# A two-layer graph attention network: TensorE takes four rows of each part of the largest tile in layer 1, and layer 2's row buffer grows from 38 to 41 rows

## The chip, the cores and the metric

The kernel runs on one core of a Trainium2 chip. The metric is the device time of one execution in microseconds (us); less is better. TensorE is written PE (its weight loads PEld), VectorE DVE, ScalarE ACT, GpSimd POOL and SyncE SP, as in the profile.

## The reference

10,000 nodes with 768 numbers each, 160,000 random edges and a loop on each node, sorted by target. Two layers of graph attention, each with a layer norm and a second product added, then a last norm over input plus output. The attention is the same in both layers; layer 1 has 4 heads of 256 numbers, layer 2 one head of 768.

```python
xl = (x @ W).reshape(n, heads, out_ch)
alpha_src = jnp.einsum('nhc,hc->nh', xl, a_src)
alpha_dst = jnp.einsum('nhc,hc->nh', xl, a_dst)
e = jax.nn.leaky_relu(alpha_src[src] + alpha_dst[dst], 0.2)
m = jax.ops.segment_max(e, dst, num_segments=n)
e = jnp.exp(e - m[dst])
s = jax.ops.segment_sum(e, dst, num_segments=n)
alpha = e / (s[dst] + 1e-16)
msg = xl[src] * alpha[:, :, None]
out = jax.ops.segment_sum(msg, dst, num_segments=n)
...
h = gat_conv(x, edge_index, W1, a_src1, a_dst1, b1, HEADS, HID, True)
h = jax.nn.relu(layer_norm(h, g1, be1)) + (h0 @ Wr1 + br1)
h1 = h
h = gat_conv(h, edge_index, W2, a_src2, a_dst2, b2, 1, OUT_DIM, False)
h = layer_norm(h, g2, be2) + (h1 @ Wr2 + br2)
```

All numbers are 32-bit floats. The output is the norm of x plus the last h.

## The kernel before

**Nodes in tiles.** The nodes are sorted by their number of edges and cut into 79 tiles of 128. A tile has as many slots as its largest node may have edges, by a rule from the sizes alone (`slot_counts`): the largest tile 41, the next 27, 26, 25 and so on down to 8. A node's edges fill its slots from the front; what is left over points at a row that adds nothing. The tiles are worked on in the order `TURNS`: every second one from the smallest up, then the others down again. By position in that order the slots are 8, 10, 11, 12, 12, 13, ... up to 26 at position 38, 41 at position 39, then 27, 25, 24, 23, 22, 22, 21, 21, 20, 20, 20, 19, 19, 19, 18, ... down to 9 at position 78. Positions 25 to 28 have 19 slots, 29 to 31 have 20, 32 and 33 have 21. There are 1,377 slots in all; `FIRST[t]` is the first slot of position t.

**The ring.** Each layer has a table of one row a node in main memory: in layer 1 the product and its logits, 1,033 numbers with the rank; in layer 2 770 numbers. One slot of one tile is fetched by one gather (L424), an indirect DMA on POOL that brings 128 rows. It lands in a ring buffer (`Ring`, L440): slot q lies in place q modulo the ring's size, 29 places in layer 1, 38 in layer 2. `fetch(upto)` issues the gathers up to a slot; after row k of a tile has been used, the loops call `fetch(FIRST[t] + k + 1 + size)`. A gather waits until the old row in its place has been read by everything that reads it. In layer 1, gathers beyond the first ring leave out slots that point at no row. In layer 2 the first slot of each tile is the tile's own rows, and is loaded from SP's queue instead (L452).

**Orders.** Both layers run under a manual schedule: each engine works through its instructions in the order in which the program writes them. So a matmul that is written later stands behind all that is written earlier for PE, and the same for the other engines and queues.

**Layer 1** (`ordered_layer1`, L667). A tile whose slots fit the ring is whole: one set of weights over all its rows (`logits`, `normalised`), then PE adds the first `ON_PE1` = 4 rows or fewer (L719: a diagonal matrix per row and head on ACT; L725: the matmul of it with the row), and DVE adds the others to the same accumulator in PSUM. Of four such rows one is multiplied and added by DVE alone (L519, four instructions, one a head), three are multiplied by ACT (L508, four instructions) and added by DVE (L515). Meanwhile PE transposes, makes the product of this tile's x (L171) and the tile before's product for layer 2 (L803). The tile at position 39 has 41 slots, more than 29, so `attend_parts` (L522) takes it in three parts of 13, 14 and 14 rows: weights of a part, the accumulator and the sum scaled down to the new maximum (L541), then its rows, one in four by DVE alone and three by ACT and DVE. PE takes no part. Before the call, `due(n)` has the rest of the tile before written out, with its product for layer 2. Next comes a division (`divided`, L435).

**Layer 2** (`ordered_layer2`, L846). In a whole tile DVE adds columns 0 to 511 of each row (L519), and PE adds columns 512 to 767 for all rows (L891: one diagonal per row on ACT, in 5 buffers of 4; L892: the matmul). PE also has the second product of each tile (`residual`, L903 and L906). The weights of the next tile are made within the loop over this one's rows, at row `turn`, and its diagonals three rows later:

```python
if t + 1 < NT and SLOTS[t + 1] + LEAD <= ring.size:
    ahead = weights_of(t + 1)
    turn = min(max(n // 3, n + SLOTS[t + 1] + 2 * LEAD - ring.size), n - LEAD)
```

`LEAD` is 3. Two norms end each tile (`norms`); their steps are taken in the loop of the following tile, at rows 0, 3, 6 and 9, and each deviation needs a square root from ACT (L565). Position 39, with 41 slots over the ring's 38, goes through `attend_parts` too: DVE adds all 768 columns of each row to an accumulator in SBUF. It is not made ahead of time in position 38, and position 40's weights are not made ahead in it.

Of the kernel before, what the change touches and what calls it, by code (L numbers as in the profile page):

```python
# [35 lines left out]
P = 128  # L36
# [8 lines left out]
LISTS = 4  # L45
G = 4
RING1 = 29
RING2 = 38
LEAD = 3
DIAGONALS = 5  # L50
ON_PE2 = 512
# [28 lines left out]
def gnn_kernel(ctx, tc, x, x_cols, src, dst, src_col, dst_col, W1, a_src1, a_dst1, b1, g1, be1, Wr1, br1,  # L80
# [423 lines left out]
    def multiply(row, e, dh):  # L504

        for h in range(e.shape[1]):
            s = slice(h * dh, (h + 1) * dh)
            nc.scalar.activation(row[:, s], row[:, s], AF.Copy, scale=e[:, h:h + 1])  # L508
# [10 lines left out]
            nc.vector.scalar_tensor_tensor(acc[:, s], row[:, s], e[:, h:h + 1],  # L519
                                           (acc if first is None else first)[:, s], op0=OP.mult, op1=OP.add)  # L520

    def attend_parts(small, ring, acc, h_, ad, bias, heads, dh, t):  # L522

        c = heads * dh
        groups = -(-SLOTS[t] * 2 // ring.size)
        cuts = [FIRST[t] + SLOTS[t] * g // groups for g in range(groups + 1)]
        top = total = None
        nc.vector.memset(acc[:, :c], 0.0)
        for lo, hi in zip(cuts, cuts[1:]):
            e, new = logits(small, ring, lo, hi, ad, heads, c, top)  # L530
            if lo == FIRST[t]:
                doubled(e, t)
            part = small.tile([P, heads], F32, name="part")
            nc.vector.reduce_sum(part, e.rearrange("p k h -> p h k"), axis=AX.X)
            if top is not None:
                fade = small.tile([P, heads], F32, name="fade")
                nc.vector.tensor_sub(fade, top, new)
                nc.scalar.activation(fade, fade, AF.Exp)
                for h in range(heads):
                    s = slice(h * dh, (h + 1) * dh)  # L540
                    nc.vector.tensor_scalar(acc[:, s], acc[:, s], fade[:, h:h + 1], None, op0=OP.mult)  # L541
                nc.vector.tensor_mul(fade, total, fade)
                nc.vector.tensor_add(part, part, fade)
            top, total = new, part
            for q in range(lo, hi):
                shared = heads > 1 and (q - lo) % SHARE
                if shared:
                    multiply(ring.slot(q), e[:, q - lo], dh)
                weigh(acc, ring.slot(q), e[:, q - lo], dh, shared=shared)
                ring.fetch(q + 1 + ring.size)  # L550
        divided(small, h_, acc, total, bias, heads, dh)
# [115 lines left out]
    def ordered_layer1():  # L667
        with tc.tile_pool(name="b1", bufs=1) as pool, tc.tile_pool(name="small1", bufs=2) as small, \
# [33 lines left out]
            def on_pe(t):  # L702


                return min(max(SLOTS[t] // 2 - 5, 1), ON_PE1, SLOTS[t])

            def weights_of(t):

                n, m = SLOTS[t], on_pe(t)
                e, _ = logits(small, ring, FIRST[t], FIRST[t] + n, ring.slot(FIRST[t])[:, C1:C1 + H1], H1, C1)  # L710
                yield e
                normalised(small, e, H1, t)

                acc = ps_acc.tile([P, 2 * BANK], F32, name="acc")
                diagonals = pool.tile([P, ON_PE1 * H1, P], F32, name="diagonals")
                for lo, hi in ((0, min(m, 2)), (min(m, 2), m)):
                    for k in range(lo, hi):
                        for i in range(H1):
                            nc.scalar.activation(diagonals[:, k * H1 + i, :], ident, AF.Copy,  # L719
                                                 scale=e[:, k, i:i + 1])  # L720
                    for k in range(lo, hi):
                        for i in range(H1):

                            c, d = i * DH1, (i + 1) * DH1
                            nc.tensor.matmul(acc[:, c:d], diagonals[:, k * H1 + i, :],  # L725
                                             ring.slot(FIRST[t] + k)[:, c:d],
                                             start=(k == 0 and c % BANK == 0),
                                             stop=(k == m - 1 and (d % BANK == 0 or d == C1)),
                                             skip_group_check=True)
                    yield acc  # L730

            def shared(t, k):
# [21 lines left out]
            for t in range(NT + 1):  # L754
                live, events = t < NT, []
                n = SLOTS[t] if live else 0
                first = done = on_pe(t) if live else 0
                whole = live and n <= ring.size
                if whole and not ready:
                    ahead = weights_of(t)  # L760
                    ready += itertools.islice(ahead, 2)

                def multiplied(upto):
                    nonlocal done
                    while whole and done < min(upto, n):
                        if shared(t, done):
                            multiply(ring.slot(FIRST[t] + done), e[:, done], DH1)
                        done += 1

                if whole:  # L770
                    e, acc = ready
                if last:
                    r_before, means = last
                    stats = deviation(small, pieces(means[:, :C1], BANK))
                for _ in ahead:
                    pass
                if full is not None:
                    store(t - 2)
                moves = []
                if live and t:  # L780
                    xT, moves = from_x(t)
                multiplied(first + 2)
                if last:
                    h = pool.tile([P, C1], F32, name="h")
                    scaled(h, [means[:, :C1]], stats, g1_b, be1_b)
                    nc.vector.scalar_tensor_tensor(h, h, 0.0, r_before[:, :C1], op0=OP.max, op1=OP.add)
                for move in moves:
                    move()
                multiplied(first + LEAD)
                if last:  # L790
                    hT = pool.tile([P, K1, P], F32, name="hT")
                    events = [(first + j, move) for j, move in enumerate(halves(hT, h))]
                if live and t:
                    r = product(xT, wr1, C1, ps_r)

                def to_layer2():
                    nonlocal full
                    nc.sync.dma_start(h1_d[t - 1], hT.rearrange("p k n -> p (k n)"))
                    full = []
                    for c in range(0, R2, BANK):  # L800
                        q = ps_half.tile([P, BANK], F32, name="half")[:, :min(BANK, R2 - c)]
                        for j in range(K1):
                            nc.tensor.matmul(q, hT[:, j, :], w2[:, j, c:c + q.shape[1]],  # L803
                                             start=(j == 0), stop=(j == K1 - 1))
                        full.append((c, q))

                if last:
                    events.append((first + 2, to_layer2))

                def next_x():  # L810
                    nonlocal xt
                    xt = fetch_x(t + 1)

                if t + 1 < NT:
                    events.append((first + 2, next_x))

                def due(k):
                    while events and events[0][0] <= k:
                        events.pop(0)[1]()

                if live and not whole:
                    due(n)
                    acc = ps_acc.tile([P, 2 * BANK], F32, name="acc")
                    ad = small.tile([P, H1], F32, name="ad")
                    nc.vector.tensor_copy(ad, ring.slot(FIRST[t])[:, C1:C1 + H1])
                    attend_parts(small, ring, acc, acc, ad, None, H1, DH1, t)
                ready = []
                ahead = iter(())
                if whole and t + 1 < NT and SLOTS[t + 1] + LEAD <= ring.size:
                    ahead = weights_of(t + 1)  # L830
                for k in range(n if whole else 0):
                    multiplied(k + 1 + LEAD)
                    if n - LEAD <= k < n - LEAD + 2:
                        ready += itertools.islice(ahead, 1)
                    if k >= first:
                        weigh(acc, ring.slot(FIRST[t] + k), e[:, k], DH1, shared=shared(t, k))
                    ring.fetch(FIRST[t] + k + 1 + ring.size)
                    due(k)
                due(DEGREES)
                ready += itertools.islice(ahead, max(2 - len(ready), 0))  # L840
                last = None
                if live:
                    last = r, acc
# [405 lines left out]
```

## Time and profile before

| what | us |
|---|---|
| timed runs, median of three | 5388.15 (5386.93 to 5388.26) |
| the profiled execution's own time | 5386.19 |
| its span | 5384.3 |
| busy: PE / PEld | 4721.3 / 2818.7 |
| busy: DVE / ACT / POOL | 4348.2 / 3138.9 / 3238.2 |
| layer 1, first to last tile (about) | 896 to 3464 |
| layer 2, first weighted row to the end (about) | 3464 to 5372 |
| position 39, layer 1: first weights to end of the division | 2121.2 to 2200.0 |
| position 39, layer 2: first weights to those of position 40 | 4395.8 to 4448.1 |

A line of the profile's groups reads: line of the program, engine, operation, what it writes and reads with shapes, how often; busy time and mean nanoseconds of one; the idle time of the engine just ahead of these, and what ended most of it. A line of an engine's queue (timeline) has the start and length in us, the same names, and in brackets the idle time before it with what ended it. Neighbours alike are merged, with their number behind an x. A line of a table by stretches has the stretch, its length, each engine's busy time with the number of instructions, the clock granted to TensorE, the share of time that the DMA engines were busy, and GB/s.

### The profile page before, as it was taken

The numbers are of one execution on the slowest core, as the hardware profiler recorded it, in microseconds if no ns is written. First come the engines' busy times: TensorE is split into PE (matmuls) and PEld (weight loads), VectorE is DVE, ScalarE is ACT, GpSimd is POOL, SyncE is SP. The second block draws the span as 40 slices with busy tenths as digits, with TensorE's granted clock in tenths as the row PEclk, the third lists the DMA queues.
The fourth block names the chain that finished last, engine by engine and source line by source line (L and its number), as shares of the span: only waits on it lengthen the run. The fifth ranks groups of instructions, "written<-read, shape, count | busy, mean of one in ns | idle before, by whom it ended". The sixth has DMA issues, their size and how long they took to land. (4 is left out here: it accounts for less than half of the span.)

```text
span 5384.3 us, 59633 instructions
## 1 busy us (share of the span) xinstructions
PE 4721.3 (88%) x15011; PEld 2818.7 (52%) x15011; DVE 4348.2 (81%) x8008; ACT 3138.9 (58%) x8204; POOL 3238.2 (60%) x3159
## 2 busy tenths in 40 slices
PE   8999996999999886478999999799988846889998
PEld 3444443555555543245555555466665534556665
DVE  5784244899999888888999999499887876878998
ACT  3434343787888877778888888344433313334443
POOL 3446455455666665556666554367776766767774
PEclk9999998999999998789999999899998978989999
DMA  4333635899999996899999998699999998999995
GB/s 155 126 98 90 90 93 202 307 338 342 359 358 369 358 346 252 306 323 355 359 365 362 350 334 303 221 327 377 369 337 327 332 301 301 341 328 354 369 382 216
DMA packets 474308, 1591.37 MB, mean 296 GB/s; under 512 B 118327, under 2 KB 122487, under 8 KB 473958
## 3 DMA queue, kind: packets, MB, share of 16 engines
q0 software_dynamic: 322384, 1286.62, 66.3%
q1 hardware_dynamic: 149520, 297.43, 16.3%
q10 hardware_dynamic: 2054, 3.42, 0.2%
q8 instruction: 126, 2.06, 0.2%
q14 instruction: 224, 1.84, 0.1%
HBM read 1431.80 MB, written 177.29 MB: 299 GB/s over the span
## 5 line engine op out<-in xcount | busy, mean ns | idle before, releaser
L424 POOL DMA_INDIRECT ring<-table,slots x2675 | 2659.6, 994 | 1486.7 <-DVE acc L519 366.4
L519 DVE SCALAR_TENSOR_TENSOR acc<-ring,e,acc 128x256 f32<-128x256 f32 (+1 forms) x2538 | 1570.8, 619 | 113.3 <-PE acc L725 37.7
L508 ACT ACTIVATE ring<-ring,e 128x256 f32<-128x256 f32 x3320 | 1351.5, 507 | 0.2
L515 DVE TENSOR_TENSOR acc<-acc,ring 128x1024 f32<-128x1024 f32 x830 | 1021.3, 1230 | 80.6 <-ACT ring L508 9.2
L171 PE MATMUL big<-w,xT 128*128 128x512 f32 x1896 | 826.1, 597 | 27.0 <-DMA w<-in_W_dram 9.6
L906 PE MATMUL big<-wr,w 128*128 128x512 f32 (+1 forms) x2528 | 846.4, 488 | 0.0
L892 PE MATMUL big<-ring,diagonals 128*128 128x256 f32 x2672 | 667.2, 412 | 193.3 <-ACT diagonals L891 180.3
L171 PE MATMUL big<-wr,xT 128*128 128x512 f32 x1896 | 835.4, 597 | 0.2 <-ACT xT L688 0.2
L803 PE MATMUL half<-w,hT 128*128 128x512 f32 (+1 forms) x2528 | 830.4, 486 | 0.0
L892 PEld LDWEIGHTS big<-ring,diagonals 128*128 128x128 f32 x2672 | 548.2, 208 | 309.8 <-ACT diagonals L891 211.8
L803 PEld LDWEIGHTS half<-w,hT 128*128 128x128 f32 x2528 | 477.8, 189 | 372.7 <-issue 310.7
L906 PEld LDWEIGHTS big<-wr,w 128*128 128x128 f32 x2528 | 482.6, 191 | 340.1 <-issue 307.5
L725 PE MATMUL acc<-ring,diagonals 128*128 128x256 f32 x1816 | 452.2, 406 | 220.5 <-ACT diagonals L719 220.2
L171 PEld LDWEIGHTS big<-w,xT 128*128 128x128 f32 x1896 | 362.5, 192 | 486.5 <-issue 467.6
L171 PEld LDWEIGHTS big<-wr,xT 128*128 128x128 f32 x1896 | 357.7, 192 | 421.6 <-issue 420.9
L725 PEld LDWEIGHTS acc<-ring,diagonals 128*128 128x128 f32 x1816 | 365.9, 204 | 299.7 <-ACT diagonals L719 242.7
L891 ACT ACTIVATE diagonals<-ident,e 128x128 f32<-128x128 f32 x1336 | 400.5, 387 | 147.6 <-DVE e L499 129.3
L565 ACT ACTIVATE sd<-mv,eps 128x1 f32<-128x1 f32 x237 | 69.8, 295 | 638.0 <-DVE mv L563 637.7
L649 DVE TENSOR_TENSOR scr<-big,ad_b 128x1024 f32<-128x1024 f32 x79 | 96.7, 1224 | 381.6 <-ACT row L646 381.6
L654 POOL TENSOR_TENSOR row<-row,none 128x1024 f32<-128x1024 f32 x79 | 187.0, 2368 | 266.8 <-ACT row L646 266.3
L719 ACT ACTIVATE diagonals<-ident,e 128x128 f32<-128x128 f32 x908 | 278.5, 387 | 117.6 <-DVE e L499 117.6
L485 ACT ACT_TABLE_LOAD x153 | 196.3, 1283 | 219.7 <-DVE e L484 108.1
(172 smaller groups left out, 3813.4 us busy)
## 6 DMA issues: line engine op xcount, KB each, us to landing
ring<-table,slots POOLq DMA_INDIRECT x2675, 6.9
table<-row SPq DMA_DIRECT2D x79, 516.0 KB, 3.7
h_d<-hT SPq DMA_DIRECT2D x79, 512.0 KB, 6.9
w<-h_d SPq DMA_DIRECT2D x79, 512.0 KB, 8.3
table<-row SPq DMA_DIRECT2D x79, 385.0 KB, 6.4
ring<-table SPq DMA_DIRECT2D x79, 385.0 KB, 6.4
xT<-in_x_cols_dram SPq DMA_DIRECT2D x79, 384.0 KB, 4.5
x_d<-xt SPq DMA_DIRECT2D x79, 384.0 KB, 6.7
```

Source lines behind the costliest of these rows:

```text
L171: nc.tensor.matmul(p[:, c:e], aT[:, j, :], w[:, j, c:e], start=(j == 0), stop=(j == k - 1))
L424: nc.gpsimd.indirect_dma_start(out=to, out_offset=None, in_=table, in_offset=bass.IndirectOffsetOnAxis(ap=index, axis=0), **more)
L485: nc.scalar.activation(e, e, AF.Exp)
L508: nc.scalar.activation(row[:, s], row[:, s], AF.Copy, scale=e[:, h:h + 1])
L515: nc.vector.tensor_add(acc[:, :c], acc[:, :c], row[:, :c])
L519: nc.vector.scalar_tensor_tensor(acc[:, s], row[:, s], e[:, h:h + 1], (acc if first is None else first)[:, s], op0=OP.mult, op1=OP.add)
L719: nc.scalar.activation(diagonals[:, k * H1 + i, :], ident, AF.Copy, scale=e[:, k, i:i + 1])
L725: nc.tensor.matmul(acc[:, c:d], diagonals[:, k * H1 + i, :], ring.slot(FIRST[t] + k)[:, c:d], start=(k == 0 and c % BANK == 0), stop=(k == ...
L803: nc.tensor.matmul(q, hT[:, j, :], w2[:, j, c:c + q.shape[1]], start=(j == 0), stop=(j == K1 - 1))
L891: nc.scalar.activation(diagonals[:, k % G, :], ident, AF.Copy, scale=e[:, k, :])
L892: nc.tensor.matmul(to, diagonals[:, k % G, :], ring.slot(FIRST[t] + k)[:, ON_PE2:C2], start=False, stop=(k == n - 1), skip_group_check=True)
L906: nc.tensor.matmul(r[:, c:d], hT[:, j, :], wr2[:, j, c:d], start=False, stop=(j == K1 - 1 and (d < C2 or not whole(t))), skip_group_check= ...
```

## The change

Four edits, three of them in layer 1 for the one tile that is taken in parts.

```diff
-RING2 = 38
+RING2 = 41
```

```diff
-    def attend_parts(small, ring, acc, h_, ad, bias, heads, dh, t):
+    def attend_parts(small, ring, acc, h_, ad, bias, heads, dh, t, summed=None):
...
             top, total = new, part
+            if summed:
+                sums, m = summed(lo, e)
+                for q in range(lo + m, hi):
+                    shared = q >= lo + m + (hi - lo - m) // 3
+                    if shared:
+                        multiply(ring.slot(q), e[:, q - lo], dh)
+                    weigh(acc, ring.slot(q), e[:, q - lo], dh, shared=shared)
+                nc.vector.tensor_add(acc[:, :c], acc[:, :c], sums[:, :c])
+                ring.fetch(hi + ring.size)
+                continue
             for q in range(lo, hi):
```

```diff
+            def summed(acc, diagonals, e, q, lo, hi, m):
+
+                for k in range(lo, hi):
+                    for i in range(H1):
+                        nc.scalar.activation(diagonals[:, k * H1 + i, :], ident, AF.Copy,
+                                             scale=e[:, k, i:i + 1])
+                for k in range(lo, hi):
+                    for i in range(H1):
+
+                        c, d = i * DH1, (i + 1) * DH1
+                        nc.tensor.matmul(acc[:, c:d], diagonals[:, k * H1 + i, :], ring.slot(q + k)[:, c:d],
+                                         start=(k == 0 and c % BANK == 0),
+                                         stop=(k == m - 1 and (d % BANK == 0 or d == C1)),
+                                         skip_group_check=True)
...
                 for lo, hi in ((0, min(m, 2)), (min(m, 2), m)):
...
+                    summed(acc, diagonals, e, FIRST[t], lo, hi, m)
                     yield acc
...
                 if live and not whole:
                     due(n)
-                    acc = ps_acc.tile([P, 2 * BANK], F32, name="acc")
+                    sums, acc = (ps_acc.tile([P, 2 * BANK], F32, name="acc") for _ in range(2))
...
-                    attend_parts(small, ring, acc, acc, ad, None, H1, DH1, t)
+
+                    def some(q, e):
+                        m = min(ON_PE1, e.shape[1])
+                        diagonals = pool.tile([P, ON_PE1 * H1, P], F32, name="diagonals")
+                        summed(sums, diagonals, e, q, 0, m, m)
+                        return sums, m
+
+                    h = pool.tile([P, C1], F32, name="h")
+                    attend_parts(small, ring, h, acc, ad, None, H1, DH1, t, some)
```

In layer 1, of each part of position 39 PE adds the first four rows into a PSUM tile of its own (`sums`); DVE takes the next three alone (9 // 3 and 10 // 3); the last six or seven go through ACT and DVE. The accumulator of these rows is now a tile in SBUF (`h`), to which DVE adds `sums` at the end of each part; the division then writes to PSUM. The part's fetches are written after all of its rows. The whole tiles' instructions are the same as before, moved into `summed`.

In layer 2 the ring's size enters the fetches, `turn` and the question which tiles are whole. With 41 places position 39 is whole: it goes through the loop of the other tiles, with PE on columns 512 to 767, and position 40's weights are made ahead in it. It is itself not made ahead in position 38 (41 + 3 > 41).

More of the change, by code (lines that the diff above doesn't have):

```diff
@@ L716, in weights_of @@
                 for lo, hi in ((0, min(m, 2)), (min(m, 2), m)):
[L717 to L729, printed above, removed]
+                    summed(acc, diagonals, e, FIRST[t], lo, hi, m)
                     yield acc
```

## The prediction

> **What bounds the kernel now.** I read the page first, then tables by stage, then the queues of single tiles. A stretch is a tile as VectorE (DVE) sees it, from the first weighted row of one tile to that of the next. "Position" is the place in the order of work; positions 0 to 78 hold 8 slots rising to 41 (position 39) and falling to 9. The page has no single bound: gathers on GpSimd (POOL), VectorE and the DMA engines share it.
>
> ```profile
> span 5384.3 us, 59633 instructions
> ...
> L424 POOL DMA_INDIRECT ring<-table,slots x2675 | 2659.6, 994 | 1486.7 <-DVE acc L519 366.4
> L519 DVE SCALAR_TENSOR_TENSOR acc<-ring,e,acc 128x256 f32<-128x256 f32 (+1 forms) x2538 | 1570.8, 619 | 113.3 <-PE acc L725 37.7
> L515 DVE TENSOR_TENSOR acc<-acc,ring 128x1024 f32<-128x1024 f32 x830 | 1021.3, 1230 | 80.6 <-ACT ring L508 9.2
> L892 PE MATMUL big<-ring,diagonals 128*128 128x256 f32 x2672 | 667.2, 412 | 193.3 <-ACT diagonals L891 180.3
> ```
>
> POOL idles 1,487 us ahead of gathers, mostly for a row buffer slot. Where that costs something only layer 2's stretches show. Columns: stretch, its length, busy time of PE, weight loads, DVE, ACT, POOL, then clock, DMA share, GB/s. Rows one to six: positions 58 (17 slots), 56 (18), 26, 27 and 52 (19), 29 (20).
>
> ```profile
> 4973.90:4995.80 21.90, 21.59 (x81) 14.88 (x80) 19.98 (x44) 9.47 (x23) 16.47 (x18) 1.00 0.99 379
> 4928.10:4951.30 23.20, 22.69 (x87) 15.97 (x86) 20.70 (x44) 9.77 (x24) 17.65 (x18) 1.00 0.99 359
> 4006.40:4033.60 27.20, 23.57 (x77) 16.28 (x77) 21.44 (x45) 10.06 (x25) 18.09 (x20) 0.87 0.91 323
> 4033.60:4061.30 27.70, 23.63 (x79) 16.36 (x78) 21.32 (x44) 10.06 (x25) 18.13 (x20) 0.88 0.90 318
> 4827.40:4854.40 27.00, 22.75 (x77) 15.64 (x77) 21.54 (x46) 10.06 (x25) 18.18 (x20) 0.87 0.92 325
> 4088.80:4117.40 28.60, 23.43 (x82) 16.36 (x81) 22.09 (x46) 10.35 (x26) 19.54 (x20) 0.88 0.91 322
> ```
>
> From 17 to 18 slots the time rises 1.3 us and DMA stays at 0.99; the nineteenth slot costs some 4 us and DMA falls to 0.91. Something opens there. In POOL's queue at position 27 it is a hole before one gather; in DVE's queue, a wait for the next tile's last row:
>
> ```profile
> 4045.43 0.95 POOL L424 DMA_INDIRECT ring<-table,slots  x1 [0.30 <-DMA ring<-table,slots]
> 4050.46 0.94 POOL L424 DMA_INDIRECT ring<-table,slots  x1 [4.09 <-DVE acc L519]
> ```
> ```profile
> 4042.45 0.15 DVE L882 TENSOR_TENSOR ad<-ring,lift 128x1 f32<-128x1 f32 x1
> 4047.97 0.19 DVE L477 TENSOR_TENSOR e<-ring,ad 128x19 f32<-128x19 f32 x1 [5.37 <-DMA ring<-table,slots]
> ```
>
> DVE stops at row `turn` until the next tile is all landed; POOL then runs until the buffer is full and stops too. Layer 1 has DVE busy 27.8 of 30.2 us in an 18-slot tile (2786.79 to 2817.02), so a shift of DVE at position 39 is carried on. There, before:
>
> ```profile
> 2132.79 10.51 PE L803 MATMUL half<-w,hT 128*128 128x512 f32 x32
> 2203.43 9.59 PE L725 MATMUL acc<-ring,diagonals 128*128 128x256 f32 x32 [60.13 <-ACT diagonals L719]
> ```
> ```profile
> 2145.12 0.21 DVE L477 TENSOR_TENSOR e<-ring,ad 128x56 f32<-128x56 f32 x1
> 2199.86 0.38 DVE L477 TENSOR_TENSOR e<-ring 128x88 f32<-128x88 f32 x2
> ```
>
> PE works for tile 38 until 2143.3; DVE ends part 1 at 2145.1 and starts position 40 at 2199.86, unheld.
>
> [...] layer 2's position 39 adds SBUF to SBUF, and gathers during its first part take 1.26 us (10.08 us for 8) against 0.95 elsewhere. [...] the trace has 1.23 with a PSUM input, and 0.95 for 768 from SBUF[...]. So I price adds into SBUF like those into PSUM.
>
> **The change, part by part.**
>
> *1. Middle tiles of layer 2, ring 38 to 41.* With n slots and n' in the next tile, turn = min(max(n//3, n+n'+6-ring), n-3), and when DVE stands at turn, POOL may run turn+ring-(n+n') rows past the next tile. Before and after: 18 slots 8 and 11; 19 slots 6 and 9; 20 slots 6 and 7; from 21 on 6 and 6 (the turn comes three rows sooner instead). At POOL's 1.25 us a gather, three rows cover 3.75 us, and the hole of 4.09 (3.79 over the usual 0.30) closes. The 18-slot row with 8 rows to spare shows it: at most 1.25 us of hole. Next is DMA: 27.7 us x 0.90/0.99 = 25.2 (2.5 less), 27.2 gives 2.2, 27.0 gives 1.9; PE's 23.6 lies below. Nine tiles (positions 24 to 28, 50 to 53) gain two or three rows: 9 x 2.2 = 20. Four of 20 slots (29, 30, 48, 49) gain one row: 4 x 1.25 = 5. Against it: at 21 slots (32, 33, 46) the turn moves from 10 to 7, where 19 and 20 slots stood before with holes of 2.7 to 4.1 us, instead of 1.33 and 2.43 at positions 32 and 33: some 1.3 x 3 = 4 lost. Sum -21; bounds -32 (holes close, DMA doesn't hold) and -8 (landings grow as the queue fills).
>
> *2. First fill.* POOL waits 5.7, 4.5 and 3.4 us at positions 1 to 3, held by PE and DVE. Three more rows are then in store when DMA becomes the limit near position 15: up to 3.75 us, taken as -3 (0 to -4).
>
> *3. Position 39 of layer 2 becomes a whole tile.* Removed: 41 adds of 1.05 us pace, the three-part exponents, and the gathers they slow. Added: 41 diagonals on ACT, 82 matmuls of 0.263 us (13.66 us for 52) = 21.6 us. New wait: its weights need all 41 rows, which fill the ring. Position 37's turn is three rows sooner, so the 5.12 us hole at 4371.46 goes and row 41 is issued near 4400, landing near 4406 (5 to 6 us as its neighbours); DVE, free at 4388, waits. Weights are out at 4409, PE starts at 4409.5. DVE adds three rows, then needs tile 38's deviation from ACT, queued behind the 41 diagonals, which PE's pace holds (20 buffers): free at row 24, 4409.5+24x0.527, +1.6, near 4424. DVE goes on at 4428. POOL stands from 4401 to 4412 and 4414 to 4429. Then 24 gathers x 1.25 and one store bring position 40's last row to 4459, landed 4463.5; DVE passes the tile's end near 4473 where it was 4457.9. But before, POOL lost 6.91 us at 4472.47 waiting for the same kind of deviation; now that hole is about 2. Measured by one gather, that of slot 747 (the 45th from position 40's first) is issued at 4482 against 4476.2 before: +6, of which the 2.8 and 1.6 us holes at positions 41 and 42 (sooner turn) give back 4. On SyncE's queue the loads for position 41 move from the tile's end to its twentieth row, so PE no longer waits for them (52.04 us idle at 4446.63 before, most of it idle anyway): nothing, since PE is not late here. Taken +2; bounds -8 and +20.
>
> *4. Layer 1, position 39.* Each part loses four rows from DVE and ACT and gets 16 diagonals x 0.305 = 4.9 us on ACT, 32 matmuls x 0.25 = 8 us on PE, one add. ACT falls in line: 16 diagonals + 6 or 7 rows x 1.61 us = 14.6 or 16.2. DVE in parts 2 and 3: 4.5 of weights, 3 x 2.17 + 7 x 1.31 and the wait for ACT's first row, +1.3 for the sums: 21.5 instead of 26.2. But part 1's matmuls stand behind tile 38's product: 2143.3 + 8 = 2151.3, so its sums are added at 2152.8, not 2145.1. Part 3 then ends at 2195.8, weights of position 40 could start at 2198.2 (-1.7). The gathers forbid that. Position 40 needs 39 of them; the first four slots now come free with PE at 2145.3 to 2151.3 (before, from 2127), 35 more at 1.34 us put the last at 2199, landing 2203; and DVE now has two SBUF inputs in each add[...]. At a third of a us each while DVE works (1.59 x 28, then 1.31) the last goes at 2207, landing 2211. So +3 to +12: taken +8. DVE waits there.
>
> The fetches, now written at the end of each part, keep their order in POOL's queue, with nothing else between them, and each still waits for its own slot: nothing. The second accumulator takes the other PSUM buffer, which tile 38's last reader (L574, 2116 to 2117) has left: nothing.
>
> Sum: -21 -3 +2 +8 = -14. On the profiled execution's 5386.2 (span 5384.3 and 1.9 around it) that is 5372; it lies 2 us under the median 5388.15 of the timed runs, so 5374.
>
> **Rivals.**
> A, the forecast, 5374: own range 5360 to 5386.
> B, a larger gain: the ring closes all holes from 18 to 27 slots. DMA's slack to 0.99 at positions 24 to 55 sums to about 65 us; with layer 1's +8 that gives 5331. For it: every hole names a freed slot. Against: from 21 slots on the rows to spare stay at 6.
> C, slower: the full ring at position 39 of layer 2. No row may be fetched until PE and DVE pass its first rows; if what follows gives nothing back, +15 at the tile's end stays, with +8 of layer 1 and only -12 of the rest: 5399. It decides from a loss of some 24 us in both tiles together. Against: holes of 6.9, 2.8 and 1.6 us that go.
> D, no change: the extra rows only lengthen the landing (8 to 10 us at DMA 0.9 already), parts 1 and 2 give 10 together, parts 3 and 4 take 10: 5388.
>
> **How the numbers follow.** Chances: A 0.45, B 0.12, C 0.20, D 0.23. The measurement tells no change from 0.2%, 10.8 us: faster is below 5377.4. Of A 0.32, of D 0.06 and all of B lie there: 0.50. Slower, above 5398.9: 0.16 of C's chance and 0.03 of D's: 0.19. Within: 0.31. The range of 8 in 10 runs from 5350 (B's nearer half) to 5400 (most of C).
>
> **What would show it.** Right: 19-slot stretches near 25 us with DMA at 0.97 or more and no hole over 1 us; 21-slot ones no shorter; POOL idle twice near position 39 of layer 2, its deviation on ACT behind diagonals; in layer 1, sums added after PE's L803, DVE waiting for gathers ahead of position 40, gathers over 1.0 us. Wrong: 19-slot tiles still at 27, 21-slot tiles shorter by 2 us, or position 40 of layer 1 starting before 2199.

## The result, and the profile after

| | us | ratio to the kernel before (95%) |
|---|---|---|
| before, six runs | 5388.24 | |
| changed, six runs | 5368.85 (5364.72 to 5373.2) | 0.9961 (0.995 to 0.9972) |
| changed, its profiled execution | 5371.7 (span 5369.8) | |

The change brings 19.4 us; 14 were foreseen. In a second set of runs, beside 5385.13 of the kernel before, it took 5361.96: ratio 0.996 (0.9947 to 0.9974).

From the page of the changed kernel, its groups (busy time and mean length, then the idle time just ahead with what ended most of it). Its lines have moved: L892 is now L913, L891 is L912, L725 is L728, L803 is L816, L519 and L424 are the same.

```profile
L424 POOL DMA_INDIRECT ring<-table,slots x2675 | 2646.8, 989 | 1468.7 <-DVE acc L519 339.9
L515 DVE TENSOR_TENSOR acc<-acc,ring 128x1024 f32<-128x1024 f32 x801 | 985.6, 1230 | 78.4 <-ACT ring L508 9.6
L913 PE MATMUL big<-ring,diagonals 128*128 128x256 f32 x2754 | 680.1, 409 | 207.7 <-ACT diagonals L912 198.0
```

POOL idles 18 us less ahead of its gathers, PE has 82 matmuls more (position 39 of layer 2), DVE 29 of its adds into PSUM fewer. The page says no more than that; where the time went is in the stretches. First three stretches of the kernel before, layer 2, columns as in the prediction: positions 32 (21 slots), 38 and 39. The border between the last two is here the first instruction of 39 on DVE, 2.8 us ahead of its first weighted row.

```profile
4174.80:4202.40 27.60, 23.14 (x83) 16.14 (x82) 23.01 (x48) 10.67 (x28) 19.99 (x22) 0.94 0.95 346
4360.70:4395.20 34.50, 33.89 (x118) 22.51 (x117) 30.15 (x53) 7.88 (x22) 22.68 (x24) 0.98 0.80 263
4395.20:4457.90 62.70, 11.27 (x25) 5.53 (x26) 51.71 (x87) 4.49 (x12) 49.55 (x44) 0.59 0.96 316
```

Then the changed kernel: positions 56 (18 slots), 26, 27 and 52 (19), 29 (20), 32 (21), 38 and 39.

```profile
4915.00:4937.40 22.40, 21.98 (x84) 15.32 (x83) 20.75 (x44) 9.76 (x24) 16.92 (x19) 1.00 1.00 371
4007.90:4032.20 24.30, 22.41 (x78) 15.39 (x77) 21.52 (x46) 10.06 (x25) 17.71 (x20) 0.93 0.97 361
4032.10:4055.30 23.20, 22.35 (x85) 15.68 (x84) 21.30 (x44) 10.06 (x25) 17.72 (x18) 1.00 0.97 361
4822.10:4846.40 24.30, 20.71 (x66) 13.82 (x65) 21.34 (x44) 10.06 (x25) 18.35 (x20) 0.86 0.99 369
4081.60:4108.80 27.20, 24.64 (x90) 17.45 (x89) 22.13 (x46) 10.35 (x26) 18.80 (x21) 0.94 0.94 339
4163.80:4193.00 29.20, 24.50 (x86) 17.24 (x85) 22.92 (x47) 10.64 (x27) 19.95 (x22) 0.88 0.91 328
4351.80:4402.70 50.90, 33.17 (x116) 21.77 (x116) 27.17 (x53) 7.41 (x17) 28.23 (x30) 0.83 0.86 249
4402.60:4466.60 64.00, 24.59 (x95) 20.27 (x94) 38.02 (x66) 20.77 (x62) 35.66 (x38) 0.66 0.72 246
```

The three tiles of 19 slots took 27.2, 27.7 and 27.0 us and take 24.3, 23.2 and 24.3: the jump behind 18 slots is gone, and the DMA share rose from between 0.90 and 0.92 to between 0.97 and 0.99. The tile of 21 slots did not get shorter: 29.2, from 27.6. POOL's queue says the same. The longest holes of the changed kernel in positions 26 and 32:

```profile
4027.03 0.97 POOL L424 DMA_INDIRECT ring<-table,slots  x1 [0.91 <-DVE acc L519]
4181.35 0.94 POOL L424 DMA_INDIRECT ring<-table,slots  x1 [3.15 <-DVE acc L519]
```

No hole in the tiles of 19 slots is over 1 us now, where each had one of 2.6 to 4.1; at 20 slots holes of 1.2 to 3.6 us are left, and at position 32 the hole of 1.33 us became 3.15. The last two rows of the table are the price: at DMA shares of 0.86 and 0.72, position 38 takes 50.9 us instead of 34.5, and position 39 doesn't get shorter by being whole.

What happens there is in the queues of the changed kernel. A line has start, length, and in brackets the idle time before it and what ended it.

```profile
4389.00 0.94 POOL L424 DMA_INDIRECT ring<-table,slots  x1 [0.30 <-issue]
4399.21 0.17 DVE L477 TENSOR_TENSOR e<-ring,ad 128x6 f32<-128x6 f32 x1 [9.40 <-DMA ring<-table,slots]
4402.00 20.02 PE L913 MATMUL big<-ring,diagonals 128*128 128x256 f32 x82 [17.73 <-ACT diagonals L912]
4404.87 0.94 POOL L424 DMA_INDIRECT ring<-table,slots  x1 [14.93 <-DVE acc L519]
4414.72 0.40 ACT L912 ACTIVATE diagonals<-ident,e 128x128 f32<-128x128 f32 x1 [0.45 <-PE big L913]
4416.44 0.30 ACT L576 ACTIVATE sd<-mv,eps 128x1 f32<-128x1 f32 x1
4416.77 0.16 DVE L587 RECIPROCAL sd<-sd 128x1 f32<-128x1 f32 x1 [10.80 <-ACT sd L576]
4421.63 0.94 POOL L424 DMA_INDIRECT ring<-table,slots  x1 [14.58 <-PE big L913]
```

Read from top to bottom: the last of 41 rows is issued at 4389.00, and the ring is full. It lands at 4399, and until then DVE has no exponents, so nothing frees a place. POOL's first stand, 14.93 us, ends with DVE's first row. Then DVE needs the deviation of position 38 from ACT; ACT has it behind the 41 diagonals, the last at 4414.72, so DVE waits 10.80 us, and POOL stands for another 14.58. The releaser named there, PE, is merely the last of several events: PE had been at work since 4402, and DVE, which reads the same places, had only come back at 4416.8.

The same for position 39 of layer 1 in the changed kernel:

```profile
2135.87 10.51 PE L816 MATMUL half<-w,hT 128*128 128x512 f32 x32
2146.22 7.08 PE L728 MATMUL acc<-ring,diagonals 128*128 128x256 f32 x32
2148.38 0.98 POOL L424 DMA_INDIRECT ring<-table,slots  x1 [21.25 <-PE acc L728]
2153.34 1.22 DVE L553 TENSOR_TENSOR h<-h,acc 128x1024 f32<-128x1024 f32 x1 [9.77 <-PE acc L728]
2161.71 2.07 POOL L424 DMA_INDIRECT ring<-table,slots  x1 [0.30 <-issue]
2170.07 1.29 POOL L424 DMA_INDIRECT ring<-table,slots  x1 [0.30 <-issue]
2204.32 0.25 DVE L477 TENSOR_TENSOR e<-ring 128x88 f32<-128x88 f32 x1 [6.43 <-DMA ring<-table,slots]
2209.82 0.18 DVE L477 TENSOR_TENSOR e<-ring 128x20 f32<-128x20 f32 x1 [5.24 <-DMA ring<-table,slots]
```

PE does tile 38's product first and the part's sums after it. So DVE waits 9.77 us to add them, and POOL 21.25 us until PE frees the first place. In the stretches where DVE adds two inputs in SBUF, nineteen of twenty gathers take 1.02 to 2.07 us, ten of them 1.24 to 1.30; the excess over 0.99 sums to 5.5 us between 2158 and 2194. DVE gets back what PE took off it and waits it out: 6.43 and 5.24 us for the rows of position 40.

By stretches the two profiled executions differ by -27.1 us in layer 2 and +6.6 in layer 1's position 39 (counted from the norm's scaling in tile 38, L574, to that in tile 39). Layer 2 begins 12.6 us later in the changed kernel's profile, 6 of it not in position 39; in the four executions with layer 1 as before that were profiled here and in experiments 2 to 4, it begins between 3457.0 and 3466.9 us, a spread of 10. So layer 1's price is read from its stretch and from runs beside each other.

### The profile page after: what moved, and what is told of

Same layout as the page of the kernel before. It is cut to its first block, busy times and chain, and to the rows that moved or that the text cites. A ratio compares the mean times of both kernels' runs of the same rounds, so it can differ in the third digit from the quotient of the medians.

```text
span 5369.8 us, 60030 instructions
## 1 busy us (share of the span) xinstructions
PE 4751.2 (88%) x15191; PEld 2846.3 (53%) x15191; DVE 4312.9 (80%) x7966; ACT 3151.9 (59%) x8255; POOL 3227.4 (60%) x3159
## 5 line engine op out<-in xcount | busy, mean ns | idle before, releaser
L424 POOL DMA_INDIRECT ring<-table,slots x2675 | 2646.8, 989 | 1468.7 <-DVE acc L519 339.9
L519 DVE SCALAR_TENSOR_TENSOR acc<-ring,e,acc 128x512 f32<-128x512 f32 (+1 forms) x2530 | 1577.7, 624 | 114.7 <-PE acc L728 39.1
L508 ACT ACTIVATE ring<-ring,e 128x256 f32<-128x256 f32 x3284 | 1337.0, 506 | 0.0
L515 DVE TENSOR_TENSOR acc<-acc,ring 128x1024 f32<-128x1024 f32 x801 | 985.6, 1230 | 78.4 <-ACT ring L508 9.6
L913 PE MATMUL big<-ring,diagonals 128*128 128x256 f32 x2754 | 680.1, 409 | 207.7 <-ACT diagonals L912 198.0
L816 PE MATMUL half<-w,hT 128*128 128x512 f32 (+1 forms) x2528 | 830.4, 486 | 0.0
L913 PEld LDWEIGHTS big<-ring,diagonals 128*128 128x128 f32 x2754 | 559.6, 206 | 325.3 <-ACT diagonals L912 228.2
L816 PEld LDWEIGHTS half<-w,hT 128*128 128x128 f32 x2528 | 477.8, 189 | 372.8 <-issue 310.7
L728 PE MATMUL acc<-ring,diagonals 128*128 128x256 f32 x1912 | 476.4, 406 | 209.4 <-ACT diagonals L722 209.0
L728 PEld LDWEIGHTS acc<-ring,diagonals 128*128 128x128 f32 x1912 | 385.3, 204 | 292.9 <-ACT diagonals L722 233.2
L912 ACT ACTIVATE diagonals<-ident,e 128x128 f32<-128x128 f32 x1377 | 412.7, 387 | 139.3 <-DVE e L499 121.2
L576 ACT ACTIVATE sd<-mv,eps 128x1 f32<-128x1 f32 x237 | 69.8, 294 | 650.4 <-DVE mv L574 650.0
L722 ACT ACTIVATE diagonals<-ident,e 128x128 f32<-128x128 f32 x956 | 292.8, 387 | 116.8 <-DVE e L499 116.5
```

The lines of the kernel that those rows point to most:

```text
L424: nc.gpsimd.indirect_dma_start(out=to, out_offset=None, in_=table, in_offset=bass.IndirectOffsetOnAxis(ap=index, axis=0), **more)
L515: nc.vector.tensor_add(acc[:, :c], acc[:, :c], row[:, :c])
L728: nc.tensor.matmul(acc[:, c:d], diagonals[:, k * H1 + i, :], ring.slot(q + k)[:, c:d], start=(k == 0 and c % BANK == 0), stop=(k == m - 1 ...
L912: nc.scalar.activation(diagonals[:, k % G, :], ident, AF.Copy, scale=e[:, k, :])
L913: nc.tensor.matmul(to, diagonals[:, k % G, :], ring.slot(FIRST[t] + k)[:, ON_PE2:C2], start=False, stop=(k == n - 1), skip_group_check=True)
```

## The experiments

Theory: the ring is the gain (rows to spare at the turn), less what position 39 gives back there, and layer 1's edit is a loss of about 7. Rivals: the edits need each other; a later turn would do as well as the ring; any 41-row tile costs this much. The twelve runs were on four chips, each beside runs of the kernel before on its own chip. On one the kernel before took 5385 us, on the others 5621 to 5648. Several expectations call the latter chips with late landings, which the traces do not bear out (end of experiment 1, and last section). Ratios are to the kernel before on the same chip; they are as on record, and can be some 0.001 off the quotient of the medians.

**1. Each edit alone** (before at 5620.89 us).

```diff
-RING2 = 38
+RING2 = 41
```

> Layer 2's ring at 41 rows, layer 1 as before. If the two halves of the change are independent and my account of them holds (layer 2 gains some 27 us in the trace after, layer 1 loses about 8): 5361 us, 19-slot tiles of layer 2 near 24 us. If the gain after is all there is in layer 2 and layer 1 cost nothing: 5369.

And the changed kernel with a ring of 38:

> The new layer 1 with a ring of 38 in layer 2. My theory (matmuls queued behind tile 38's product free the slots late, gathers slowed by VectorE's two SBUF inputs, position 40 waits for gathers): slower by 7 to 10 us, 5396. Rival (the faster parts 2 and 3 win, and the later start of layer 2 in the trace is scatter): 5386 or less.

Measured: the ring alone 5655.68, ratio 1.0051 (1.0031 to 1.0071), slower; layer 1's edit alone 5626.92, 1.0006 (0.9995 to 1.0017). The first is a miss, in sign too; the second lies on the expected side, but can't be told from no change. In the profile of the ring alone layer 1 is as before (position 39 takes 88.4 us), and layer 2 starts at 3467.5. But layer 2 itself, 1894 us in the changed kernel's first profile, takes 2191. Positions 26, 27, 38 and 39 of the ring alone on this chip, columns as above:

```profile
4078.70:4109.30 30.60, 25.82 (x77) 17.07 (x76) 21.59 (x46) 10.27 (x27) 18.04 (x20) 0.83 0.88 289
4109.30:4141.20 31.90, 27.58 (x81) 17.85 (x80) 21.47 (x45) 10.31 (x27) 18.97 (x21) 0.82 0.86 284
4475.10:4532.20 57.10, 40.23 (x142) 27.08 (x142) 27.11 (x52) 8.97 (x22) 29.74 (x32) 0.86 0.80 238
4532.20:4597.20 65.00, 25.66 (x98) 21.19 (x97) 38.03 (x66) 21.07 (x62) 35.82 (x38) 0.64 0.70 243
```

DVE and POOL are busy for as long as in the changed kernel's profile (21.5 and 18 us), yet these tiles of 19 slots take 31 us: 284 to 289 GB/s where 361 were moved there, at DMA shares of 0.86 to 0.88 where it was 0.97. The ring's gain is missing (positions 24 to 28 take 144.6 us, against 154.9 and 142.7 in the two kernels with 38 rows and the turn unmoved on this chip), and positions 38 to 42 take 250.7 against 223.2 and 227.5: the ring filled to its last row costs some 25 us.

DVE waits for other engines there. One form of PE's matmuls of the second product (L906) and DVE's longest waits between 3700 and 5200 us: first of the ring alone on the chip at 5385 (experiment 2), then on this one. A line of waits has the total, the number of times and the longest, in us; "remote" is an event for which the profile shows no instruction.

```profile
L906 PE MATMUL big<-wr,w 128*128 128x256 f32 x944 | 213.4, 379 | 0.0
DVE e L477 <- DMA ring<-table,slots: 147.9, 36, 13.5
```
```profile
L906 PE MATMUL big<-wr,w 128*128 128x256 f32 x752 | 218.1, 421 | 111.7 <-issue 110.1
DVE sd L576 <- ACT sd L565: 116.3, 12, 11.8
DVE st L561 <- remote: 112.3, 15, 15.3
DVE st L561 <- PE big L906: 68.0, 10, 12.0
DVE e L477 <- DMA ring<-table,slots: 82.8, 18, 13.3
```

On this chip PE stands ahead of these matmuls for 111.7 us in all, nearly all of it with nothing shown that it waits for; on the other it never does. DVE waits most for what the norms need: columns that PE finishes (L561), and the deviation from ACT (L576), which stands in ACT's order behind diagonals whose buffers PE frees. For gathered rows it waits less than on the other chip. That fits the missing gain, though no run tests it: the ring closes a hole of POOL, and here DVE is held by PE. The split of the first result is left open by this, so the comparison was repeated.

**2. The same beside the changed kernel, on the chip at 5385.13.**

> The changed kernel itself, once more, beside the parts of it. If this chip's kernel before takes about 5388: 5369 (0.9964). If it takes about 5620 as in the first set of experiments, where rows of layer 2 land late: the ring's cost there (ratio 1.005) and layer 1's (1.0005) say about 1.0055, that is slower; the rival, that the two edits help each other, says below 1.003 there.

> Ring of 41 rows alone. Theory (ring gains about 27 in layer 2, layer 1's edit costs about 7 plus what scatters): 0.27 to 0.34 of the kernel before less per cent, that is 5359 to 5365 where before takes 5388. Rival (layer 1's edit has part in the gain): no better than the changed kernel, 5369 or more. On a chip with late landings: ratio 1.003 to 1.007 again, because position 39 taken whole makes POOL stand for 14 to 16 us three times.

Measured: changed 5361.96, 0.996 (0.9947 to 0.9974); the ring alone 5353.4, 0.9943 (0.993 to 0.9957). The ring gives 31.7 us, layer 1's edit takes 8.6 back. That the edits need each other is out. Of the 31.7 us the profile finds 27.9 in layer 2 (1892.8 us, from 1920.7); the rest lies in the scatter of what comes before.

**3. A ring of 40: spare rows without the whole position 39.**

```diff
-RING2 = 38
+RING2 = 40
```

> Ring of 40 rows: tiles of 19 slots have 8 rows to spare at their turn instead of 6, and position 39 stays in parts. If the gain is the spare rows and position 39 taken whole gives back (about 7 over positions 37 to 42 on the first chip, more where landings are late): 4 to 10 us faster than the ring of 41 on a chip like the first, 5350 to 5357, and not slower than before (ratio at most 1.001) on a chip with late landings. Rival (two or three more rows of ring are harmful by themselves on a chip with late landings, e.g. because turns move to other slots): the same ratio as the ring of 41, within 0.001.

Measured beside them: 5353.7, 0.9947 (0.9934 to 0.9961): no faster than 41, a miss. The stretches say why. Positions 37 to 42 take 239.3 us against 254.2 with 41 (and 248.6 before): what position 39 gives back is real, 15 us. But the others give up as much: positions 24 to 31 take 5.4 us more than with 41 rows, 43 to 53 7.2 more. The 41st place is worth some 12 us outside positions 37 to 42, which spend it. By size of tile: with 40 rows the seven tiles of 19 slots, most with 8 rows to spare, gain 15.5 us (18.4 with 41, where most have 9); the four of 20 that precede another of 20, with 6 to spare as before, gain nothing (0.5 us longer, against 4.6 shorter with 41, where they have 7).

**4. Position 38's norm ahead of position 39's weights, ring of 41.**

```diff
+                    if not ready and t:
+                        for _ in last:
+                            pass
                     e = (ready or list(weights_of(t)))[0]
```

> Ring of 41 rows, and position 38's normalisation issued whole before the weights of position 39, so that its deviation on ScalarE is no longer behind a row's diagonals. Theory (the second stand of POOL at position 39, 14.6 us, comes from the multiplications of position 39 waiting for position 38's rows of the ring to be freed late behind that normalisation): 5 to 14 us faster than the ring of 41 alone. Rival (the stand is set by the last row's landing at 4399 and the tile's own 41 rows of work, whatever the order of the norms): within 3 us of the ring of 41 alone.

Measured beside the last three: 5344.25, 0.9923 (0.991 to 0.9937), 9.2 us under the ring alone. By stretches layer 2 is 18.4 us shorter than in the profile of the ring alone, but begins 9.9 later, behind a layer 1 with the same instructions; so the stretches say more of this edit than the medians. Positions 38 and 39, first with the ring alone, then with the norms first:

```profile
4332.80:4383.00 50.20, 33.43 (x117) 21.98 (x116) 27.16 (x52) 7.42 (x17) 28.27 (x30) 0.84 0.85 254
4383.00:4447.70 64.70, 25.21 (x95) 20.77 (x94) 38.01 (x66) 20.87 (x62) 35.69 (x38) 0.66 0.71 244
```
```profile
4340.80:4389.80 49.00, 31.56 (x110) 20.39 (x108) 32.05 (x62) 7.89 (x16) 29.55 (x31) 0.86 0.89 267
4389.80:4439.10 49.30, 24.66 (x98) 20.57 (x99) 33.67 (x55) 17.56 (x60) 34.75 (x37) 0.72 0.88 311
```

Position 39 falls by 15.4 us. From the queues of the kernel with the norms first:

```profile
4372.38 0.17 DVE L919 RECIPROCAL sd<-sd 128x1 f32<-128x1 f32 x1 [0.42 <-ACT sd L565]
4387.52 0.17 DVE L477 TENSOR_TENSOR e<-ring,ad 128x6 f32<-128x6 f32 x1 [8.94 <-DMA ring<-table,slots]
4389.87 10.62 ACT L891 ACTIVATE diagonals<-ident,e 128x128 f32<-128x128 f32 x36 [1.20 <-DVE e L499]
4390.60 25.30 DVE L519 SCALAR_TENSOR_TENSOR acc<-ring,e,acc 128x512 f32<-128x512 f32 x32
4392.67 0.97 POOL L424 DMA_INDIRECT ring<-table,slots  x1 [12.10 <-PE big L892]
```

The norm is done at 4372 to 4374, in the time in which DVE waits for landings anyway. So DVE runs 32 rows on end from 4390.60. The edit moves the whole norm: of the 15.4 us some 4 are DVE's own work on it, done ahead now (busy 33.67 in position 39, from 38.01), the rest is the wait for ACT. The first stand of POOL stays (12.10 us), the second is gone: it belonged to the norm that waits behind the diagonals, not to a 41-row tile as such.

**5. Layer 1 with its rows gathered in PSUM** (before at 5620.89). The changed kernel with a ring of 38; ACT copies the sums to a tile in SBUF (`moved`), so that DVE adds one input from SBUF and one from PSUM.

```diff
-                nc.vector.tensor_add(acc[:, :c], acc[:, :c], sums[:, :c])
+                nc.scalar.copy(moved[:, :c], sums[:, :c])
+                nc.vector.tensor_add(acc[:, :c], acc[:, :c], moved[:, :c])
...
-                    h = pool.tile([P, C1], F32, name="h")
-                    attend_parts(small, ring, h, acc, ad, None, H1, DH1, t, some)
+                    attend_parts(small, ring, acc, acc, ad, None, H1, DH1, t, some)
```

> As the new layer 1 with a ring of 38, but VectorE adds the rows into PSUM; ScalarE copies PE's sums to SBUF at the end of each part. If two SBUF inputs of VectorE slow the gathers: gathers back at 0.99 us, position 40 starts about 5 us sooner than with the new layer 1 alone, 5391. If only the late slots count: 5396, as with the new layer 1 alone.

Measured: 5624.64, 1.0001 (0.9988 to 1.0015); in time it can't be told from layer 1's edit as it stands. In the trace it can. From POOL's queue:

```profile
2154.23 0.99 POOL L424 DMA_INDIRECT ring<-table,slots  x1 [21.21 <-PE acc L729]
2167.19 0.99 POOL L424 DMA_INDIRECT ring<-table,slots  x1 [0.30 <-issue]
```

All of the part's gathers take 0.99 us, the long ones are gone, and position 39 falls from 94.8 (layer 1's edit alone) to 93.1 us; some 5 were expected. POOL's wait for PE is as long as ever (21.21), so most of the price is not the gathers' length.

**6. The product of tile 38 behind the part's sums, too** (before at 5648.3). As 5, and:

```diff
                 if live and not whole:
+                    product_later = events.pop([f for _, f in events].index(to_layer2))
                     due(n)
+                    events.append(product_later)
```

> Layer 1's edit on a ring of 38 rows, with VectorE's rows gathered in PSUM and the product of tile 38 issued after the parts' sums. The changed kernel minus the ring alone (5362.0 and 5353.4) puts layer 1's edit at plus 8.6 us. Theory (nearly all of that is TensorE's sums standing 10.5 us behind that product, and the gathers slowed by sums of two SBUF inputs): both gone, position 39 ends earlier than with four scaled rows on VectorE, its stretch 79 to 83 us where the old layer 1 takes 88.4 and the changed one 94.9, and the time is 5 to 10 us under the kernel before (ratio about 0.9985). Rival (the 41-row tile stands on the arrival of its last part's rows whatever TensorE does first): stretch above 88, ratio 1.000 to 1.002.

From its queues:

```profile
2142.55 7.09 PE L729 MATMUL acc<-ring,diagonals 128*128 128x256 f32 x32
2144.72 0.99 POOL L424 DMA_INDIRECT ring<-table,slots  x1 [10.16 <-PE acc L729]
2150.72 1.23 DVE L554 TENSOR_TENSOR acc<-acc,h 128x1024 f32<-128x1024 f32 x1 [0.53 <-ACT h L553]
2185.29 10.51 PE L817 MATMUL half<-w,hT 128*128 128x512 f32 x32
```

PE takes the sums as soon as it can and the product 43 us later, which delays nobody; POOL's wait falls from 21.2 to 10.2 us, DVE's for the sums to half a microsecond. Position 39 takes 82.7 us, against 88.4 before and 94.9 in the changed kernel. The time is 5644.73, ratio 0.9992 (0.9981 to 1.0003): 4 us in the expected direction, where 5 to 10 were expected, by itself not told from none; the stretch is what decides between theory and rival here.

**7. A later turn in place of more rows** (before at 5620.89, then 5648.3).

```diff
-turn = min(max(n // 3, n + SLOTS[t + 1] + 2 * LEAD - ring.size), n - LEAD)
+turn = min(max(n // 3, n + SLOTS[t + 1] + 3 * LEAD - ring.size), n - LEAD)
```

> Before with a ring of 38, but the turn three rows later (9 rows to spare past the next tile instead of 6 wherever the formula rules). My theory, that rows to spare at the turn are what the ring bought: 19-slot tiles fall from 27 to about 25 us, 20- to 23-slot tiles lose most of their hole too; 5345 to 5360. Rival, that it is the size of the ring: no gain, 5388 or slower, since the next tile's diagonals come later.

> Ring of 38 rows, with the turn to the next tile put three rows later, so that 19-slot tiles have 9 rows to spare there, as with 41 rows. Theory (the gain of the ring is rows to spare at the turn, and the turn may pay for them as well as the ring): positions 24 to 28 and 51 to 53 give 15 us or more of the 22 they gave with 41 rows, and position 39 gives nothing back: 5360 to 5372 where before takes 5385. Rival (a later turn takes from the next tile's start what it gives at this one's end, so that only rows of the ring count): not under 5380.

With a ring of 41 and the norms first:

> Ring of 41 rows, position 38's normalisation before the weights of position 39, and the turn three rows later. If spare rows at the turn still pay at 20 to 23 slots, where POOL's holes of 1 to 3 us are left: 5 to 15 us under the 5344 of the ring of 41 with the norms first (ratio 0.990 or less). Rival (a later turn costs the next tile's start): the same 5344 or slower, ratio 0.992 to 0.996.

Measured: 5662.45, 1.0066 (1.0048 to 1.0084); again 5687.08, 1.0062 (1.0042 to 1.0082); with 41 rows and the norms first 5667.02, 1.0035 (1.0025 to 1.0045). Misses, but all three on chips of the kind on which the ring's spare rows brought nothing in experiment 1. The stretches don't decide it: in the first run positions 24 to 28 take 136.0 us (154.9 and 142.7 with the turn unmoved on that chip), but 50 to 53 take 130.2 (117.9 and 119.2); in the second they take 148.1 and 120.9 (146.4 and 121.9). Whether a later turn gains where the ring does stays open.

**8. Both losses taken out** (before at 5647.73): the changed kernel with 4, 5 and 6.

> The changed kernel with both of its losses taken out: in layer 1 VectorE's rows gathered in PSUM and tile 38's product after the parts' sums (worth 12 of the 94.9 us that position 39 takes in the changed kernel), in layer 2 position 38's normalisation ahead of the weights of position 39 (worth 15 of its 64). If both losses are what the traces showed, the two add up: 5335 to 5345 where before takes 5385 (ratio 0.991 to 0.9925), against 5362 of the changed kernel, and the stretches of position 39 are 81 to 84 us in layer 1 and 48 to 51 in layer 2. Rival (the losses come back as a later wait): 5350 or more. On a chip where rows of layer 2 land late (before at 5620 to 5650): ratio 1.001 to 1.004, since 41 rows at once cost about 12 us over positions 38 to 40 there even with the norms first, and the spare rows gain nothing.

Measured: 5644.08, ratio 0.9991 (0.9982 to 1.0), a little better than expected of such a chip. Its position 39 in layer 1, then in layer 2:

```profile
2124.30:2208.25 83.95, 52.49 (x168) 36.10 (x169) 66.42 (x132) 56.42 (x150) 41.65 (x42) 0.78 0.60 211
4533.40:4585.50 52.10, 29.05 (x95) 22.47 (x96) 33.65 (x56) 17.56 (x60) 34.76 (x37) 0.70 0.85 294
```

Both repairs hold in one kernel: 84.0 us for 94.9, 52.1 for 64.0. What it would take where the kernel before takes 5385 wasn't measured. The best that was is experiment 4: 5344.25, against 5385.13 before and 5361.96 changed.

## Why the prediction was right, step by step

The forecast was 5374, the result 5368.85. Measured by stretches; layer 2 is the mean of three profiled executions with 41 rows (the changed kernel twice, the ring alone of experiment 2) against the one of before.

| step | foreseen | measured |
|---|---|---|
| 1: nine tiles at positions 24 to 28, 50 to 53 | -20 | -23.7 |
| 1: four of 20 slots | -5 | -4.9 |
| 1: three of 21 slots | +4 | +4.5 |
| 2: first fill (positions 0 to 23) | -3 | -7.2 |
| 3: position 39 of layer 2 (37 to 42) | +2 | +5.9 |
| 4: position 39 of layer 1 | +8 | +6.6 (8.6 between medians) |
| not foreseen: positions 54 to 61 | 0 | -4.2 |
| other positions | 0 | +1.1 |
| sum | -14 | -21.9 |

The medians of the two sets give -19.4 and -23.2 for the whole. That the sum came so near is in part luck: steps 2 and 3 were each wrong by some 4 us, in opposite directions.

*Step 1* was right in mechanism and size. POOL's hole closed, DMA rose to 0.97 and more, and the 21-slot tiles lost what the sooner turn cost; the nine tiles took 22.7 to 26.2 us, where 25.2 was worked out from 27.7 x 0.90 / 0.99. That it is the rows to spare is supported by the ring of 40, whose gains follow them by size of tile; the direct test, the later turn, fell on chips of the kind on which the ring gained nothing either.

*Step 2* was right in sign and too small. The term counted POOL's three rows in store, at most 3.75 us. Positions 15 to 17 alone became 6.6 us shorter (22.4 us a tile to 20.2, near the 19.9 of positions 62 to 64, which have the same slots). Part comes back at position 19 (+2.7). Why a tile gains more than the rows in store is not settled, nor what positions 54 to 61 gain, which the forecast put at nothing.

*Step 3* was right in every wait that it named: the last row, the two stands of POOL (foreseen 11 and 15 us, measured 14.93 and 14.58), the deviation behind the diagonals. Two terms were mis-sized. The last row was given 5 to 6 us to land and took 10. And position 40 was to have a hole of about 2 us left where it has 2.8 and 4.2. So positions 38 and 39 together took 17.5 us more instead of 15, and their neighbours gave back 11.6 where 13 were counted. Experiment 4 shows the second stand to be that of the norm behind the diagonals: with the norm ahead, position 39 is 15.4 us shorter.

*Step 4* was right. The sums behind tile 38's product, DVE's wait for position 40's rows and the lengthened gathers are all in the trace; experiments 5 and 6 took them away one after the other. The product in front costs most (94.9 to 82.7 with both, 1.7 of it the gathers'). The excess of the gathers was put at some 9 us (a third of a us for 28, an estimate from the 1.26 us of layer 2's position 39 before, against 0.95 elsewhere) and measures 5.5.

*The rivals.* C's mechanism was real, but took 12.5 us in the two tiles at position 39 where it needed some 24 and a smaller gain elsewhere; the ring alone is slower only on a chip where PE stands within layer 2 (1.0051). B failed as argued: 21-slot tiles still stand with the same six rows to spare (the hole of 3.15 us). Of D the losses were there (12.5 for 10), but parts 1 and 2 gave 31 us, not 10.

## What to carry to other kernels

A larger buffer paid here where the producer's hole named a freed slot, and only until the next limit was met: the 19-slot tiles went from between 27.0 and 27.7 us to between 23.2 and 24.3, at a DMA share of 0.97 or more; the 21-slot tile went from 27.6 to 29.2. So count rows to spare for each size of tile, and compare with a neighbour that has more. In experiment 1, where DVE waited 116.3 us for deviations from ACT and 68.0 us for PE's second product, more rows brought nothing (ratio 1.0051). The tile that fills the buffer to the last row made its producer stop until its first use (14.93 us); before letting one do so, move everything that its consumer owes to the tile before (here a square root) ahead of the wait: in experiment 4 that took 15.4 us off position 39, some 4 of them DVE's own work done earlier. Work moved onto an idle engine is only early if nothing is queued there in front of it: PE's sums stood behind a product of 10.51 us, and DVE waited 9.77 us for them; with the product behind them (experiment 6) it waited 0.53.

## What the runs showed of the hardware that was not expected

- The kernel before takes 5385 to 5388 us in two sets of runs and 5621 to 5648 on three other chips. The difference is in layer 2: it starts at 3457 to 3484 us on all of them, and with 38 rows and the turn unmoved lasts 1920.7 us in the first profile and 2135 to 2160 there. The trace shows it on PE. Of the 2,528 matmuls of the second product none stands for more than 0.15 us in the six profiles of the first two sets; in the eight from the other chips 87 to 155 do, for 107 to 163 us in all. The packets of the gathers differ little: in layer 2 their median is 235 ns before and in the ring alone at 5656 us, and the slowest hundredth takes 874 and 939 ns or more.
- TensorE's clock was granted at one half for 245 to 301 us of layer 2 in the six profiles and for 478 to 538 in the eight; in layer 1 for 273 to 294 and 277 to 311. In the ring alone at 5656 us, 60 of the 163 us of PE's stops lie in half-clock stretches as recorded, and 130 if the stretches are taken 3.4 us (one step of the clock's record) earlier; they have about a quarter of layer 2. With that shift, which no run tests, the half clock mostly comes just behind a stop. In the six profiles the 245 to 301 us of half clock come without any of these stops. What makes PE stand on these chips, and in layer 2 more than in layer 1, stays open.
- Gathers took longer while DVE added two SBUF inputs: in layer 1's position 39 of the changed kernel nineteen of twenty took 1.02 to 2.07 us, from 0.99, and all are back at 0.99 with the accumulator in PSUM (experiment 5). What in the two slows them is not shown.
- Scaling the 1,024 columns of the accumulator by four numbers (L542 in the changed kernel, four instructions) takes 1.15 and 1.41 us in SBUF, and 2.08 in PSUM (L541 before).
